# Block 1's second product ahead of block 0's feed-forward, and block 0's tokens turned by VectorE and DMAs

## The chip, the cores and the metric

The kernel runs on one core of a Trainium2 chip. Its time is the device time of that core in microseconds (us), and the time given is a median of several runs. A profiled execution gives a span, which is the time between the first and the last event on the core, and a trace of each instruction.

The core's engines are named as in the profile. PE is TensorE, with PEld for its weight loads. DVE is VectorE. ACT is ScalarE. POOL is GpSimd. SP is SyncE, and it only issues DMAs. ACT issues some DMAs too. A name with q (SPq, ACTq) is the queue of DMA issues of that engine. [...]

## The reference, cut to what matters

```
emb = silu(t) @ ada_w + ada_b
shift_msa, scale_msa, gate_msa, shift_mlp, scale_mlp, gate_mlp = split(emb, 6)
norm  = ln(x) * (1 + scale_msa) + shift_msa
x     = x + gate_msa * (gelu(norm @ ssm_w1 + ssm_b1) @ ssm_w2 + ssm_b2)
norm2 = ln(x) * (1 + scale_mlp) + shift_mlp
x     = x + gate_mlp * (gelu_tanh(norm2 @ ff_w1 + ff_b1) @ ff_w2 + ff_b2)
```

x is 2 x 2048 tokens of 512 features, in float32. ssm_w1 and ssm_w2 are 512 x 512, ff_w1 is 512 x 1024 and ff_w2 is 1024 x 512. ada_w is 512 x 3072. t has one row per batch, so the shifts, scales and gates are one vector per batch.

## The kernel before

**Blocks and stages.** The 4096 tokens are cut into eight blocks of 512. A block i passes four products on PE. hA_i is norm @ ssm_w1 with its GELU (`First`). oA_i is the product with ssm_w2 and the addition to x (`residual`). hC_i is norm2 @ ff_w1 with its GELU (`Second`). oC_i is the product with ff_w2 and the second addition to x, again through `residual`.

**Seven products instead of eight.** Every one of these multiplications is done by a Strassen-Winograd scheme on quarters of the operands. The seven products are called P1 to P7, and the function `group` issues them in the order P1, P2, P6, P5, P7, P3, P4. For a few early stages the order is `FIRST`, that is P1, P2, P5, P6, P7, P3, P4. Several products accumulate into one PSUM bank: P1, P6, P7 and P4 share bank y, P5 and P3 share bank v, and P2 has bank x. VectorE has to read a bank between two of them, by the addition in `residual` or in `hidden`. So PE can't start P6 before VectorE has read P1, nor P7 before it has read P6, nor P4 before P7, nor P3 before P5.

**Sums.** The scheme needs sums of quarters. They are steps on operands in SBUF:

- the sums of normalized tokens, written to tiles nS (`Norm.summed`, lines 319 to 322)
- the sums of hidden values, hSA for hA and hSC for hC (lines 309 to 312)
- the sums of weights, w_s and fw_s, which are also lines 309 to 312 for first operands and 319 to 322 for second ones. The weights w2 and fw2 are first multiplied by the gate (line 353, "fold").

The blocks 1 to 7 do hC in another way, called `products`: 26 products in place of 28, from 28 operands made of ff_w1 (the list HK_A, 37 steps on VectorE) and 24 operands made of the tokens (the list HK_B, 20 steps on POOL, the tile forms). Both lists are worked out by line 635. The list HK_A is worked out once, after hC_0 has read the plain weights and they have been loaded again. I call its steps the fw sums, and the 20 others the forms.

**Tokens on their way to PE.** A product needs features on partitions, while x has tokens there. Statistics come from VectorE (lines 419 and 420), the scales from eight small POOL steps (lines 428 to 446), and the normalization from ACT (line 459). Then there are two ways to turn the tokens. In the first, PE transposes them into PSUM (line 488) and ACT or VectorE applies shift and scale (lines 502 and 504). In the second, VectorE transposes blocks of 32 x 32 (`turn`, line 470), sixteen DMAs move the blocks (`move`, line 479), and ACT applies shift and scale to what arrived. In the kernel before, block 0's tokens go the first way for hA_0 and hC_0, block 1's for hA_1. All others go the second way.

**Order.** The order on each engine is the order of the code. Side work is put into `hooks`: a dictionary that lists, for a product such as P5, the steps to emit after it. The order of the stages on PE is

```
hA_0, oA_0, hA_1, hC_0, oA_1, oC_0, hA_2, products(1), oA_2, oC_1, hA_3, products(2), ...
```

Biases (line 610) are additions of a bias row to x on POOL. `load_x`, `load_ada` and `load_w` put loads on SP's queue, but the second load of ff_w1 is on ACT's. Large tiles (x, nT, hA, hC and the ada weights) share eight buffers.

Of the kernel before, what the change touches and what calls it, by code (L numbers as in the profile page):

```python
# [140 lines left out]
def kernel(  # L141
# [111 lines left out]
    def modulation(g0, part):  # L253


        g = g0 + part
        pa = ps_g.tile([P, D], F32, tag="x", name=f"pada_{g}")
        w = ada[g].rearrange("p k (n m q) -> p k m n q", n=KD, q=G)
        for k in range(KD):
            for m in range(P // G):  # L260
                nc.tensor.matmul(
                    pa[m * G : (m + 1) * G, :P],
                    silu[:, k, :],
                    w[:, k, m],
                    start=(k == 0),
                    stop=(k == KD - 1),
                    tile_position=(0, m * G),
                    skip_group_check=True,
                )
        turned = work.tile([P, KD, G], F32, tag="turned", name=f"turned_{g}")  # L270
        nc.vector.transpose(turned.rearrange("p n q -> p (n q)"), pa[:, :P])
        m = const.tile([P, KD, B], F32, tag=f"mod_{g0}_{part}", name=f"mod_{g0}_{part}")
        bias = colsT[:, R_ADA + g * KD : R_ADA + (g + 1) * KD]
        nc.vector.tensor_tensor(m, turned[:, :, :B], bias.unsqueeze(2).to_broadcast([P, KD, B]), ALU.add)
        mods[g0, part] = m
# [130 lines left out]
    class Norm:  # L406
# [68 lines left out]
        def move(self, engs=(nc.sync,)):  # L475

            for a in range(C):
                for m in range(C):
                    engs[m % len(engs)].dma_start(
                        out=self.nT[m * Q : (m + 1) * Q, a, :],  # L480
                        in_=self.bl[a * Q : (a + 1) * Q, m].rearrange("p k c q -> p (k c q)"),
                    )
# [174 lines left out]
    class Second:  # L657
# [9 lines left out]
        def products(self, fa, fb, hooks):  # L667
# [13 lines left out]
            def dest(d):  # L681
                f, col = d // 2, d % 2
                h = (self.lo, self.hi)[f // 2]
                return h[:, 2 * (f % 2) : 2 * (f % 2) + 2, col * HT : (col + 1) * HT]
# [9 lines left out]
            for n, (b, fresh, ra, rb, reads) in enumerate(HK_P):  # L694
# [9 lines left out]
                for d, sign in reads:  # L704
                    if d not in fresh_dest:
                        op = ALU.add if sign > 0 else ALU.subtract
                        nc.vector.tensor_tensor(dest(d), dest(d), ps[b], op)  # L707
                for d, sign in reads:
                    if d in fresh_dest:
                        nc.scalar.activation(dest(d), ps[b], AF.Identity, scale=float(sign))  # L710
                        fresh_dest.discard(d)
# [119 lines left out]
    hook(hooks, ("P1",), st[2:] + [n1[1].scales] + fold2(7, 8))  # L831
    hook(hooks, ("P2",), hA_sums[2:] + [lambda c=c: n1[1].normal(c, on_pe=True) for c in range(C)])
# [4 lines left out]
    hook(hooks, ("P3",), st[:2])  # L837
    residual("oA_0", 0, hA[0], w2_ops, KD // 2, hooks, order=FIRST)
    fw1_ops, fw1_sums, fw1_s = weight_of_first("fw1", fw1_sb)
    run(fw1_sums)  # L840
    n1_sums = n1[1].summed(nc.vector)
    run(n1_sums[:3])

    hooks = {}
    hook(hooks, ("P1",), st[2:] + [n2[0].scales])
    hook(hooks, ("P2",), [lambda c=c: n2[0].normal(c, on_pe=True) for c in range(C)])
    hook(hooks, ("P2",), biases(1, gb[2]))
    hook(hooks, ("P5",), n1_sums[3:])
    hook(hooks, ("P6",), [lambda: rows_of_gates(5)])
    hook(hooks, ("P3", "P3", "P4", "P4"), n2[0].turned((1, 3)))  # L850
# [19 lines left out]
    first_hooks = {}  # L870
    hook(first_hooks, ("P1",), [ff_gate])
    hook(first_hooks, ("P1", "P2"), n2_sums[2:])
    hook(first_hooks, ("P6", "P5", "P7", "P3"), fold5(0, 4))
    fold = None


# [3 lines left out]
    fb, fa_sums = {}, []  # L880
# [6 lines left out]
    n1[2] = Norm(2, 1)  # L887
    for i in range(NBLK):
        nxt, nx2, last = i + 1 < NBLK, i + 2 < NBLK, i + 1 == NBLK
        hC = Second(i)  # L890
        if i == 0:
            hooks = first_hooks
            hook(hooks, ("P2",), hA[1].summed(nc.gpsimd))
            hook(hooks, ("P2", "P3", "P4"), n1[2].stats())
            hC.group(0, n2[0].ops, hooks)
            hooks = {}
            hook(hooks, EARLY, hC.summed(0, nc.gpsimd))
            hook(hooks, ("P1",), [n1[2].scales])
            hook(hooks, EARLY, [lambda c=c: n1[2].normal(c) for c in range(C)])
            hook(hooks, ("P7", "P3", "P3", "P4"), [lambda c=c: n1[2].turn(c) for c in range(C)])  # L900
            hook(hooks, ("P4",), [n1[2].move])
            hook(hooks, ("P1", "P2", "P6", "P5"), fold5(4, 8))
            hook(hooks, ("P7",), fold5(8, 12) + [gb5_0] + biases(0, gb[5]))
            hC.group(1, n2[0].ops, hooks)
            fw2_ops = found["fw2"][0]
        else:
            hooks = {}
            if i == 1:
                hook(hooks, range(0, 26), take(len(fa_sums)))
            if i == 1:  # L910
                hook(hooks, (0,), [n1[i + 2].scales])
            if nxt:
                hook(hooks, (1, 2, 3, 4), hA[i + 1].summed(nc.gpsimd))
            hook(hooks, (6, 7, 8, 9), biases(i, gb[5]))
            if nx2:
                hook(hooks, (12, 14, 16, 18), [lambda c=c: n1[i + 2].normal(c) for c in range(C)])
                hook(hooks, (14, 16, 18, 20), [lambda c=c: n1[i + 2].turn(c) for c in range(C)])
                hook(hooks, (20,), [n1[i + 2].move])
            if fold:
                hook(hooks, (2, 6, 23, 25), fold[:4])  # L920
            hook(hooks, (20,), hC.summed(0, nc.gpsimd))
            hC.products(fa, fb[i], hooks)
# [3 lines left out]
        if nxt:  # L926

            if i == 0:
                hook(hooks, ("P1",), [lambda: load_w("fw1", fw1, fw1_sb, nc.scalar)])
                fa_sums.extend(sums_of_registers(HK_A, fa, (nc.vector,)))  # L930
# [24 lines left out]
        if i == 0:  # L955
            hook(hooks, ("P1",) * 6 + ("P5",) * 7 + ("P7",) * 7 + ("P3",) * 2, take(22))
        elif i + 3 < NBLK:
            hook(hooks, ("P5", "P7", "P3", "P4"), n1[i + 3].stats())
            hook(hooks, ("P4",), [n1[i + 3].scales])
# [11 lines left out]
        if nxt:  # L971
            hook(hooks, ("P7",) if nx2 else ("P5",), n2[i + 1].moved((None,) if nx2 else (None, nc.vector)))
# [34 lines left out]
        if i == 0:  # L1007
            hook(hooks, ("P5", "P7", "P3", "P4"), n1[i + 3].stats())
            hook(hooks, ("P1", "P2", "P2", "P6", "P5", "P7", "P3"), take(7))
# [50 lines left out]
```

## Time and profile before

| | |
|---|---|
| median of 3 runs | 608.73 us |
| lowest and highest | 607.0 and 609.22 us |
| profiled execution, its own time | 607.58 us |
| its span | 605.8 us |
| granted TensorE clock | 1.0 over the whole span |
| PE busy | 593.8 us, 98% |
| VectorE busy | 370.9 us, 61% |
| POOL busy | 394.7 us, 65% |
| ACT busy | 214.8 us, 35% |

The profiled execution is 1.15 us shorter than the median, and its time is 1.8 us more than its span. In the profile a group of instructions is written as line, engine, operation, out<-in with the shape, a count, then the busy time, the mean of one in ns, and the idle time before it with what ended it. In a timeline a row starts with its start and its duration in us. A matmul of this kernel is counted twice in the profile, so a product of four matmuls shows as x8. The tile names leave numbers out: fw stands for ff_w1 and ff_w2, w for ssm_w1 and ssm_w2, forms for the tile of token sums.

### The profile page before, as it was taken

The page shows a single profiled execution, that of the slowest core. Times are in us where ns is not written, and L with a number is a line of the kernel's source. Part 1 is how long each engine was busy: PE and PEld are TensorE (multiplying, and loading weights), DVE is VectorE, ACT ScalarE, POOL GpSimd, SP SyncE. Part 2 cuts the span into 40 slices and gives each one's busy share as a digit, 9 for nine tenths or more (in the row PEclk, how much of TensorE's full clock was granted, in tenths as well). Part 3 has the DMA queues.
Part 4 walks back from the last instruction along what each step waited for, and adds up shares of the span by engine and source line. Part 5 has one row for each costly group of instructions (what it writes and reads, how often), then busy time and mean ns, then how long its engine had stood idle before and what let it go on. Part 6 is the DMA issues. An engine that isn't in the chain of part 4 may idle for free.

```text
span 605.8 us, 8128 instructions
## 1 busy us (share of the span) xinstructions
PE 593.8 (98%) x2843; PEld 511.2 (84%) x2843; DVE 370.9 (61%) x638; ACT 214.8 (35%) x355; POOL 394.7 (65%) x446
## 2 busy tenths in 40 slices
PE   7999999999999999999999999999999999999997
PEld 4777888887888888888888888888888888888886
DVE  5987786799754375555754458644565346457642
ACT  3233340424622354323631346113553234212420
POOL 2876489889635797539978398885984695540110
PEclk9999999999999999999999999999999999999999
DMA  8980006410133103440042511321020300012001
GB/s 324 413 341 1 1 19 206 124 69 1 45 96 87 54 2 79 148 136 4 1 138 64 185 50 28 112 70 70 1 61 10 104 36 0 1 46 94 1 0 70
DMA packets 22604, 49.85 MB, mean 82 GB/s; under 512 B 4084, under 2 KB 4640, under 8 KB 21668
## 3 DMA queue, kind: packets, MB, share of 16 engines
q1 hardware_dynamic: 19264, 43.53, 21.3%
q10 hardware_dynamic: 3300, 5.80, 3.5%
q8 instruction: 23, 0.38, 0.3%
q14 instruction: 17, 0.14, 0.1%
HBM read 27.29 MB, written 8.39 MB: 59 GB/s over the span
## 4 chain that ended last, share of the span: by engine, by line
PE 86%; DVE 8%; DMA 2%; issue 1%; ACTq 1%; ACT 1%; POOL 0%; SPq 0%; DVEq 0%
PE py_oC L385 15%; PE px_hC L696 9%; PE py_oA L385 9%; PE py_hA L385 8%; PE pv_hC L696 8%; PE pv_oC L385 7%; PE py_hC L696 7%; PE pv_oA L385 4%; PE pv_hA L385 4%; PE px_oC L385 4%; PE py_hC L385 2%; PE px_oA L385 2%; PE px_hA L385 2%; DMA ada<-in_L_cond_ada_w_dram 2%; PE pv_hC L385 1%
## 5 line engine op out<-in xcount | busy, mean ns | idle before, releaser
L610 POOL TENSOR_TENSOR x<-x,gb 128x512 f32<-128x512 f32 x64 | 80.1, 1285 | 5.9 <-issue 2.1
L502 ACT ACTIVATE nT<-nT,mod,mod 128x512 f32<-128x512 f32 x50 | 36.7, 802 | 123.1 <-DMA nT<-blocks 114.7
L428 POOL TENSOR_SCALAR ve<-mv 128x4 f32<-128x4 f32 x16 | 3.8, 236 | 86.5 <-DVE mv L420 80.4
L459 ACT ACTIVATE nT<-x,nmr,rstd 128x512 f32<-128x512 f32 x52 | 39.6, 803 | 54.7 <-POOL nmr L446 38.9
L385 PE MATMUL py_oC<-fw_s,hSC 128*128 128x256 f32 x256 | 57.9, 379 | 0.0
L385 PEld LDWEIGHTS py_oC<-fw_s,hSC 128*128 128x128 f32 x256 | 48.6, 190 | 6.6
L309 POOL TENSOR_TENSOR hSC<-hClo 128x512 f32<-128x512 f32 x15 | 19.1, 1277 | 48.7 <-ACT hClo L691 38.9
L419 DVE BATCH_NORM_STATS2 st<-x 128x6 f32<-128x512 f32 x64 | 43.4, 677 | 5.0 <-DMA x<-in_x_dram 4.7
L598 DVE TENSOR_TENSOR x<-py_oC,x 128x512 f32<-128x512 f32 (+1 forms) x36 | 22.6, 630 | 37.6 <-PE py_oC L385 37.2
L696 PE MATMUL py_hC<-forms,fw 128*128 128x256 f32 x168 | 41.1, 380 | 0.0
L707 DVE TENSOR_TENSOR hClo<-hClo,py_hC 128x512 f32<-128x512 f32 x42 | 28.6, 681 | 16.9 <-ACT hClo L710 9.1
L470 DVE STREAM_TRANSPOSE blocks<-nT 128x512 f32<-128x512 f32 x52 | 35.2, 694 | 5.2 <-ACT nT L459 4.8
L635 POOL TENSOR_TENSOR forms<-forms 128x256 f32<-128x256 f32 x48 | 35.8, 747 | 2.8
L696 PEld LDWEIGHTS py_hC<-forms,fw 128*128 128x128 f32 x168 | 31.8, 190 | 4.7 <-DVE hClo L707 0.4
L598 DVE TENSOR_TENSOR x<-py_oA,x 128x512 f32<-128x512 f32 x32 | 22.1, 690 | 21.2 <-PE py_oA L385 19.6
L707 DVE TENSOR_TENSOR hChi<-hChi,pv_hC 128x512 f32<-128x512 f32 x35 | 23.3, 683 | 16.9 <-PE pv_hC L696 16.9
L385 PE MATMUL py_oA<-w_s,hSA 128*128 128x256 f32 x128 | 30.4, 380 | 0.8 <-DVE hSA L311 0.8
L385 PE MATMUL py_hA<-nS,w_s 128*128 128x256 f32 x128 | 30.4, 380 | 0.6 <-DVE hA L559 0.6
L691 ACT ACTIVATE hClo<-hClo,colsT 128x256 f32<-128x256 f32 x56 | 25.3, 500 | 13.6 <-DVE hClo L707 13.5
L385 PE MATMUL py_oC<-fw_s,hChi 128*128 128x256 f32 x128 | 29.0, 380 | 0.6 <-DVE x L598 0.6
L385 PE MATMUL px_oC<-fw,hChi 128*128 128x256 f32 x128 | 28.9, 379 | 0.0
L385 PE MATMUL pv_oC<-fw,hSC 128*128 128x256 f32 x128 | 28.9, 379 | 0.0
(224 smaller groups left out, 1426.0 us busy)
## 6 DMA issues: line engine op xcount, KB each, us to landing
nT<-blocks SPq DMA_DIRECT2D x152, 64.0 KB, 2.0
out_dram<-x SPq DMA_DIRECT2D x15, 512.0 KB, 3.0
x<-in_x_dram SPq DMA_DIRECT2D x7, 1024.0 KB, 6.3
ada<-in_L_cond_ada_w_dram SPq DMA_DIRECT2D x6, 1024.0 KB, 9.5
fw<-in_L_cond_ff_w_dram SPq DMA_DIRECT2D x3, 2048.0 KB, 9.3
nT<-blocks ACTq DMA_DIRECT2D x56, 64.0 KB, 2.2
w<-in_L_cond_ssm_w_dram SPq DMA_DIRECT2D x3, 1024.0 KB, 8.4
fw<-in_L_cond_ff_w_dram ACTq DMA_DIRECT2D x1, 2048.0 KB, 9.6
```

Of the source, the lines that this page charges most:

```text
L309: lambda: eng.tensor_tensor(s[1], q["11"], q["21"], ALU.subtract),
L385: nc.tensor.matmul(ps[b][j * apart][:, j, :], lhs(p, j, k), rhs(p, j, k), start=(fresh and j * (not apart) == 0 and k == 0), stop=(p in (" ...
L419: nc.vector.bn_stats(st, xs[self.i][:, c, :])
L459: nc.scalar.activation(t, x_c, AF.Identity, bias=self.nmr[:, c : c + 1], scale=self.rstd[:, c : c + 1])
L470: nc.vector.transpose(self.bl[:, :, :, c, :].rearrange("p m k q -> p k m q"), self.nT[:, c, :].rearrange("p (k m q) -> p k m q", k=KD, m=C),)
L502: nc.scalar.activation(dst, src, AF.Identity, bias=shift, scale=scale)
L598: nc.vector.tensor_tensor(d, ps[BANK[p]][:, js], d, ALU.add)
L610: lambda c=c: nc.gpsimd.tensor_tensor(xs[i][:, c, :], xs[i][:, c, :], gb, ALU.add)
L635: eng.tensor_tensor(reg[d], reg[a], reg[b], ALU.add if f == "+" else ALU.subtract)
L691: nc.scalar.activation(h, h, AF.Gelu_apprx_tanh, bias=fb1T[:, m : m + 1])
L696: nc.tensor.matmul(ps[b][:, j, :], fa[ra][:, j * P : (j + 1) * P], fb[rb].rearrange("p a (c q) -> p c a q", q=Q), start=(fresh and j == 0) ...
L707: nc.vector.tensor_tensor(dest(d), dest(d), ps[b], op)
```

## The change

The order of the first stages on PE becomes

```
hA_0, oA_0, hA_1, oA_1, hC_0, hA_2, oC_0, products(1), oA_2, oC_1, hA_3, products(2), ...
```

so oA_1 precedes hC_0, and hA_2 precedes oC_0. Block 0's second tokens go the second way: VectorE turns them in hA_1, SP and ACT issue eight moves each, and ACT applies shift and scale in oA_1. Their sums nS go from VectorE to POOL. The side work of these stages is hooked anew: two of the four ff_w1 sums on POOL run in oA_0 and the other two behind block 1's biases in hA_1. The statistics of block 1 for its second normalization run in hC_0, the multiplication of ff_w2 by its gate runs in hC_0 too, and its sums on POOL in hA_2. The second load of ff_w1 is issued at the start of hA_2, and of the 37 fw sums 4 are in hA_2, 29 in oC_0 and the last 4 in products(1). Before, 22 were in oC_0, 7 in hA_2 and 8 in products(1).

There are three smaller edits. `modulation` lets VectorE write the turned rows into PSUM instead of SBUF. `products` has a parameter `last`: in the last block ACT takes its fresh reads of a bank before VectorE's. And in the last block the shift and scale of the four token parts is hooked behind P5 and P7 in turn, where all four were behind P5.

```diff
-        turned = work.tile([P, KD, G], F32, tag="turned", name=f"turned_{g}")
-        nc.vector.transpose(turned.rearrange("p n q -> p (n q)"), pa[:, :P])
+        turned = pa[:, P : 2 * P]
+        nc.vector.transpose(turned, pa[:, :P])
+        turned = turned.rearrange("p (n q) -> p n q", n=KD)
...
-        def move(self, engs=(nc.sync,)):
+        def move(self, engs=(nc.sync,), part=range(C)):
...
-                for m in range(C):
+                for m in part:
...
+                fresh_reads = [r for r in reads if r[0] in fresh_dest]
+                other_reads = [r for r in reads if r not in fresh_reads]
+                fresh_dest -= {d for d, _ in fresh_reads}
+                for turn in (fresh_reads, other_reads)[:: 1 if last else -1]:
...
-    hook(hooks, ("P1",), st[2:] + [n1[1].scales] + fold2(7, 8))
-    hook(hooks, ("P2",), hA_sums[2:] + [lambda c=c: n1[1].normal(c, on_pe=True) for c in range(C)])
+    hook(hooks, ("P1",), hA_sums[2:3] + st[2:] + [n1[1].scales] + fold2(7, 8))
+    hook(hooks, ("P2",), hA_sums[3:] + [lambda c=c: n1[1].normal(c, on_pe=True) for c in range(C)])
...
+    fw1_ops, fw1_sums, fw1_s = weight_of_first("fw1", fw1_sb)
+    hook(hooks, ("P2",), fw1_sums[:1])
+    hook(hooks, ("P5",), fw1_sums[1:2])
     residual("oA_0", 0, hA[0], w2_ops, KD // 2, hooks, order=FIRST)
-    fw1_ops, fw1_sums, fw1_s = weight_of_first("fw1", fw1_sb)
-    run(fw1_sums)
     n1_sums = n1[1].summed(nc.vector)
-    run(n1_sums[:3])
+    run(st[2:3] + n1_sums[:2] + st[3:])
     hooks = {}
-    hook(hooks, ("P1",), st[2:] + [n2[0].scales])
-    hook(hooks, ("P2",), [lambda c=c: n2[0].normal(c, on_pe=True) for c in range(C)])
-    hook(hooks, ("P2",), biases(1, gb[2]))
-    hook(hooks, ("P5",), n1_sums[3:])
+    hook(hooks, ("P1",), n1_sums[2:3] + [n2[0].scales])
+    hook(hooks, ("P2",), n1_sums[3:] + [lambda c=c: n2[0].normal(c) for c in range(C)])
+    hook(hooks, ("P2",), biases(1, gb[2]) + fw1_sums[2:])
     hook(hooks, ("P6",), [lambda: rows_of_gates(5)])
-    hook(hooks, ("P3", "P3", "P4", "P4"), n2[0].turned((1, 3)))
+    hook(hooks, ("P6", "P6", "P7", "P7"), [lambda c=c: n2[0].turn(c) for c in range(C)])
+    hook(hooks, ("P7",), [lambda: n2[0].move((nc.sync,), (0, 1))])
...
+    n2[0].move((nc.scalar,), (2, 3))
+    hA_sums = hA[1].summed(nc.vector)
+    run(hA_sums[:2])
+    n1[2] = Norm(2, 1)
+    st = n1[2].stats()
+    hooks = {}
+    hook(hooks, ("P1",), hA_sums[2:3])
+    hook(hooks, ("P2",), hA_sums[3:])
+    hook(hooks, ("P2", "P6", "P6", "P5"), st)
+    hook(hooks, ("P5",), [n1[2].scales])
+    hook(hooks, ("P6",), n2[0].moved())
+    hook(hooks, ("P5",), [ff_gate])
+    hook(hooks, ("P7",), n2[0].summed(nc.gpsimd) + [lambda c=c: n1[2].normal(c) for c in range(C)])
+    turns = [lambda c=c: n1[2].turn(c) for c in range(C)]
+    residual("oA_1", 1, hA[1], w2_ops, KD // 2, hooks)
+    hC = Second(0)
...
+    hook(hooks, ("P1",), [gb5_0] + biases(0, gb[5]))
+    hook(hooks, ("P1", "P1", "P2"), turns)
+    hook(hooks, ("P2",), [n1[2].move])
+    hook(hooks, ("P3", "P4"), fold5(0, 2))
+    hC.group(0, n2[0].ops, hooks)
+    hooks = {}
+    hook(hooks, ("P1", "P1", "P2", "P6"), hC.summed(0, nc.gpsimd))
+    hook(hooks, ("P2",), n1[2].moved())
+    hook(hooks, ("P6",), n1[2].summed(nc.gpsimd))
+    hook(hooks, ("P1", "P2", "P6", "P5"), n2[1].stats())
+    hook(hooks, ("P5",), [n2[1].scales])
+    hook(hooks, ("P1", "P2", "P6", "P5", "P7", "P3"), fold5(2, 8))
+    hC.group(1, n2[0].ops, hooks)
...
+    hook(hooks, ("P1",), [lambda: load_w("fw1", fw1, fw1_sb, nc.scalar)])
+    hook(hooks, ("P1",), fold5(8, 12) + hC.summed(1, nc.gpsimd))
+    hook(hooks, ("P2", "P6", "P6", "P5"), [lambda c=c: n2[1].normal(c) for c in range(C)])
+    hook(hooks, ("P5", "P7", "P3", "P4"), [lambda c=c: n2[1].turn(c) for c in range(C)])
+    hook(hooks, ("P4",), [lambda: n2[1].move((nc.sync, nc.scalar))])
+    hook(hooks, ("P3", "P3", "P4", "P4"), take(4))
+    hA[2] = First(2, n1[2].ops, hooks)
...
+    hook(hooks, ("P1",), [lambda: load_x(3)] + take(5))
+    hook(hooks, ("P1",), n2[1].moved() + biases(2, gb[2]))
+    fb[1] = n2[1].registers()
+    hook(hooks, ("P2", "P6"), sums_of_registers(HK_B, fb[1], (nc.gpsimd,)))
+    hook(hooks, ("P2",) * 6 + ("P6",) * 5 + ("P5",) * 6 + ("P7",) * 4 + ("P3",) * 3, take(24))
+    hook(hooks, ("P5", "P7", "P3", "P4"), n1[3].stats())
+    residual("oC_0", 0, hC, fw2_ops, KH // 2, hooks)
...
-            hook(hooks, ("P7",) if nx2 else ("P5",), n2[i + 1].moved((None,) if nx2 else (None, nc.vector)))
+            moved = n2[i + 1].moved((None,) if nx2 else (None, nc.vector))
+            hook(hooks, ("P7",) if nx2 else ("P5", "P7", "P5", "P7"), moved)
```

## The prediction

> **What bounds the kernel now.** I read the page's busy shares and its chain first, then who made TensorE (PE) wait, then the engines' timelines over the first 175 us, which is where the change lies.
>
> ```profile
> PE 593.8 (98%) x2843; PEld 511.2 (84%) x2843; DVE 370.9 (61%) x638; ACT 214.8 (35%) x355; POOL 394.7 (65%) x446
> PE 86%; DVE 8%; DMA 2%; issue 1%; ACTq 1%; ACT 1%; POOL 0%; SPq 0%; DVEq 0%
> ```
>
> PE is the bound; only its own work and its waits count. The waits (line, waited-for, us in total, times, longest):
>
> ```profile
> PE py_oA L385 <- DVE hSA L311: 0.8, 1, 0.8
> PE px_hC L696 <- DVE hChi L707: 0.7, 2, 0.5
> PE px_hC L696 <- ACT hClo L710: 0.7, 1, 0.7
> PE pv_hA L385 <- DVE nT L320: 0.6, 1, 0.6
> PE py_oC L385 <- DVE x L598: 0.6, 1, 0.6
> PE py_hA L385 <- DVE hA L559: 0.6, 1, 0.6
> ```
>
> All but the ACT one and one of px_hC (the last block, 560 us) fall before 150 us. So little can be won: these waits and the PE transposes. PE's timeline (start, us):
>
> ```profile
> 59.55 1.07 PE L488 MATMUL pt<-ident,blocks 128*128 128x128 f32 x8
> 60.46 1.89 PE L385 MATMUL py_hA<-nS,w 128*128 128x256 f32 x8
> 62.19 1.04 PE L488 MATMUL pt<-ident,blocks 128*128 128x128 f32 x8
> 63.06 1.89 PE L385 MATMUL py_hC<-nT,fw 128*128 128x256 f32 x8
> ```
>
> Start to start, a product of hA, oA or hC takes 1.73 us (oC 3.45), and block 0's second transposes 0.91 + 0.87 = 1.78 us. What can be lost is seen where VectorE (DVE) and GpSimd (POOL) both read two operands from SBUF:
>
> ```profile
> 46.99 2.36 POOL L312 TENSOR_TENSOR fw_s<-fw,fw_s 128x1024 f32<-128x1024 f32 x1
> ```
>
> ```profile
> 47.66 2.24 DVE L319 TENSOR_TENSOR nS<-nT 128x512 f32<-128x512 f32 x1 [1.08 <-ACT nT L502]
> ```
>
> ```profile
> 113.98 5.49 POOL L610 TENSOR_TENSOR x<-x,gb 128x512 f32<-128x512 f32 x4
> ```
>
> ```profile
> 114.27 0.69 DVE L598 TENSOR_TENSOR x<-pv_oC,x 128x512 f32<-128x512 f32 x1 [1.62 <-PE pv_oC L385]
> 114.87 2.07 DVE L635 TENSOR_TENSOR fw_s<-fw_s,fw 128x256 f32<-128x256 f32 x2
> 116.97 1.37 DVE L635 TENSOR_TENSOR fw_s<-fw,fw_s 128x256 f32<-128x256 f32 x1
> 118.38 1.37 DVE L635 TENSOR_TENSOR fw<-fw,fw_s 128x256 f32<-128x256 f32 x1
> 119.79 0.42 DVE L635 TENSOR_TENSOR fw<-fw 128x256 f32<-128x256 f32 x1
> ```
>
> The DVE step on nS (0.69 alone) ended when POOL's did. Of the fw sums DVE got one done per POOL instruction, and 0.42 us once POOL was idle; a read from PSUM (L598, 0.69) was not held.
>
> **Early part.** The instruction order of both kernels gives DVE's sequence; I move the starts of the trace by it. In oA_0 the third DVE sum of hA (L311) goes ahead of two statistics: the 0.94 us gap before P6 goes, but block 1's scales, and with them its four normalizations on ACT (38.50 to 41.43), come 0.6 later, so PE waits at the first transpose instead and is 0.5 late there. POOL no longer runs the fw1 sums at 47 us, so nS is free by 49.5: the 0.80 gap before pv_hA goes (net -0.3), and DVE has read P6's bank by 54.7, when PE is still at the gate's rows (53.9 to 54.8): the 0.84 gap before P7 goes (net -1.1). Without the transposes hA_1 ends at 60.0 instead of 63.06: **-3.0**. The turn of the four ada modulations in PSUM costs PE nothing (their L274 takes 0.17 us alone, 1.15 and 2.37 beside POOL; what waits next there is ACT or the lock anyway).
>
> **The new tokens' path.** Statistics end at 50.4, POOL's scales take 3.2, ACT normalizes 53.6 to 56.5, DVE turns (0.65 each) until 58.8. Then 16 moves, half on SP, half on ACT. The issue rows:
>
> ```profile
> 89.19 14.27 SPq L479 DMA_DIRECT2D nT<-blocks  x16
> 112.67 5.23 SPq L479 DMA_DIRECT2D nT<-blocks  x8
> 159.04 10.44 SPq L479 DMA_DIRECT2D nT<-blocks  x16
> ```
>
> ACT's eight queue behind the last GELU of hA_1 (61.1); 5.4 of issue and 1.7 to land give 68.2, four modulations 71.2. hC_0 starts 13 us after 60.0 (oA_1's seven products and the gate's 0.86), so PE isn't held: no charge; late by over 4 us it would be one for one. The Trainium skill ("VectorE: DVE Perf Modes", Rules for kernel authors) says to transpose 128x128 on TensorE where PSUM will do. By it the change loses a 12 us path for 1.78 us of PE; by the rows that path is covered here, and the 1.78 is won. SP's x_2 load is now ahead of these moves, unblocked earlier, and free.
>
> **oA_1.** Its P6 needs two DVE sums of hA_1 after u2's GELU at 60.1. POOL, after biases (53.6 to 58.5), now runs the two late fw1 sums, 2.4 us each, until 63.3. One DVE step per POOL step: the first ends 61.5, the second 64.5, then an addition and the third sum, 65.8, against 63.5 wanted: **+2.3** (0 without the lock). hC_0: POOL's sums of nT reach s0 at 78.85, PE 78.8, and DVE has 2.0 us of work per 1.73 us product in group 1: +0.3.
>
> **hA_2 and oC_0, the main term.** Block 2's 16 moves leave on SP at 81.7, 11.8 us to modulation (as at 159: 171.1), 93.5 to 96.5. In order, POOL then has: sums of nT (to 101.9), scales of block 1 (105.1), the fw2 sums, 4 x 2.4 (114.9), four hSC sums (120.8), four biases (126.5), 20 forms at 0.86 (143.8; before 16.57 us in all). PE runs hA_2 from 99.8 to 111.9 and would end oC_0 at 136. So POOL is never idle in it, and DVE now has 33 fw sums there (4 in hA_2, 5 behind oC_0's P1, then 6, 5, 6, 4, 3), 22 before. These are ahead of the additions (L598) which read PSUM before PE may accumulate into the bank again. Rows of these sums:
>
> ```profile
> L635 DVE TENSOR_TENSOR fw<-fw 128x256 f32<-128x256 f32 x11 | 7.7, 696 | 0.0
> L635 DVE TENSOR_TENSOR forms<-forms 128x256 f32<-128x256 f32 x8 | 3.4, 421 | 0.2
> ```
>
> The third field is busy time in us and the mean in ns. Two totals can be made. By the mean row, 0.70 each, 15 sums from 111.4 and three other steps (1.9) put the addition of P6 at 123.8, before P7 wants the bank at 125.7; the next eleven, an addition and a statistic put that of P7 at 133.8, P4 wanting 132.6: **+1.2**. By the Trainium skill ("SBUF — State Buffer", Who interferes with whom): a DVE instruction with two SBUF inputs contends with a GpSimd one that reads SBUF, and the loser waits out the winner's whole instruction; so one sum per POOL step, 2.45, 1.37 or 0.86 us each. Laid side by side: two sums wait out fw2 steps (115.3), then a turn; two go with hSC steps 1 and 2, P1's addition ends at 119.0 (P6 wants the bank at 118.8, +0.3); five go with hSC 3, 4 and biases 1 to 3 (125.4), P2's addition, six with bias 4 and forms 1 to 5 (131.3), so P6's addition ends at 131.9 (P7 wants it at 126.0, **+6.0**); five with forms 6 to 10, P5's addition 136.2 (P3: +0.9); six with forms 11 to 16 (140.8), a statistic, P7's addition 142.2 (P4: 139.7, **+2.5**). Together +9.7. I take this: the mean row mixes free and held sums, and the timeline above has the strict form wherever POOL was busy. Both ends stay in the range. The fw1 load, now issued by ACT at 101, lands 9.6 later (its row's median), just before DVE's first fw sum at 111.4; what it is later, DVE is later.
>
> Gone in exchange is the 0.76 gap before the last oC_0 product and 0.2 of smaller ones: -1.0. products(1) then starts at 145.7 (137.41 before: -3.0 + 2.3 + 0.3 + 9.7 - 1.0 = +8.3). Its own stalls were 1.9; DVE is late into it: 2 to 3.5, +1.0.
>
> **The last block.** ACT reads a fresh bank before DVE: ACT no longer waits for hChi (its 0.60 at 560.04 starts near 557.5), and half the modulations move behind P7's addition, in DVE's idle time, so forms end 0.6 sooner. The gaps of 0.82 and 0.45 at 560 to 562 go: **-1.2**; at worst one stays.
>
> **Sum.** +8.3 + 1.0 - 1.2 = +8.1. The profiled execution took 607.58 (span 605.8), 1.15 under the median 608.73: 615.7 on the one, 616.8 on the other; I say **616**.
>
> **Rivals.** *(1) Strict lock*, above: 616, own range 612 to 620. *(2) The lock bites partly*: nT of block 1 comes later than 126, POOL idles before the forms and DVE clears its sums at 0.42: with oC_0 stalls of 4 to 5 the sum is +2.4 to +3.4, with the mean row's 1.2 it is -0.4: 606 to 612. *(3) DVE's backlog doesn't reach PE*: -3.0 + 2.3 + 0.3 - 1.0 - 0.5 (fewer stalls in products) - 1.2 = -3.1, and near -5.5 without oA_1's hold: 603 to 605.6. For it: the transposes are sure, and a sum takes 0.42 where POOL idles; against it: the four held rows at 114 us. It decides if P6's addition ends within 3.45 us of P6's end. *(4) The moves are late*: 14.3 for 16 on SP, as at 89 us beside the fw load: nT sums reach s0 1.6 us after hA_2's P6 wants it, and POOL's whole queue follows, about +10: 618 to 620; against it, the fw1 load is now behind these moves.
>
> **Chances.** 0.5% (3.0 us) is about what a measurement tells from no change. (1) 0.56 and (4) 0.08 make slower 0.64; (2) 0.18; (3) 0.18. The range 604 to 620 leaves out a little over half of (3) and the upper edge of (4); most of the chance lies in 612 to 620.
>
> **What would show it.** Right: PE waits of several us on py_oC before P7 and P4 of the first oC, released by DVE's L598 addition; DVE's fw sums there near 0.9 to 1.4 us; a 2 us wait of py_oA for hSA near 64 us; no px_hC wait in the last block. Wrong: fw sums near 0.42 in oC_0, or the first oC without gaps; then it is faster, and the POOL queue was free where I have it full.

## The result and the profile after

The changed kernel took 616.74 us (median; 614.97 to 617.31), the kernel before 607.90 beside it on the same chip. The ratio is 1.0139, 95% interval 1.0107 to 1.0170. The change costs 1.4%. The profiled execution of the changed kernel took 614.97 us with a span of 613.2, against 607.58 and 605.8 before. The three other runs, 616.3 to 617.31 us, had a mean granted clock of 0.992 and the profiled one 0.994, so what follows is read from a run that is 1.8 us under the median.

The page's busy shares, then its chain:

```profile
PE 594.4 (97%) x2827; PEld 510.8 (83%) x2827; DVE 379.0 (62%) x641; ACT 216.6 (35%) x357; POOL 394.6 (64%) x445
PE 84%; DVE 10%; issue 2%; DMA 2%; POOL 1%; ACT 1%; SPq 0%; POOLq 0%; DVEq 0%; ACTq 0%
```

PE issues 16 matmul rows fewer (the transposes) and is still the bound. But the span grew by 7.4 us while its busy time grew by 0.6, and VectorE's part of the chain went from 8% to 10%. So nearly all of the time went into waits. PE's waits, in the columns used for the kernel before:

```profile
PE py_oC L386 <- DVE x L599: 7.4, 3, 5.6
PE py_oA L386 <- DVE hSA L312: 2.0, 1, 2.0
PE px_hC L698 <- ACT hClo L712: 0.8, 1, 0.8
PE py_hC L386 <- POOL nS L322: 0.2, 1, 0.2
```

The first line is the addition of oC_0 (L599 now, L598 before). PE's timeline shows where the 7.4 us are. The rows are P6, P5, P7, P3 and P4 of oC_0:

```profile
119.58 3.69 PE L386 MATMUL py_oC<-fw_s,hSC 128*128 128x256 f32 x16 [0.21 <-DVE x L599]
123.11 3.62 PE L386 MATMUL pv_oC<-fw,hClo 128*128 128x256 f32 x16
132.28 5.33 PE L386 MATMUL py_oC<-fw_s,hSC 128*128 128x256 f32 x16 [5.55 <-DVE x L599]
137.44 3.62 PE L386 MATMUL pv_oC<-fw,hSC 128*128 128x256 f32 x16
142.74 3.72 PE L386 MATMUL py_oC<-fw_s,hChi 128*128 128x256 f32 x16 [1.68 <-DVE x L599]
```

P7 waits 5.55 us for P6's addition and P4 1.68 us for P7's. P7 itself also takes 5.16 us from its start to P3's, where the other products take 3.45 to 3.55. VectorE's rows ahead of P6's addition, which is the L599 at 131.54, and the two additions after it, P5's at 135.94 and P7's at 142.02:

```profile
121.69 2.79 DVE L636 TENSOR_TENSOR fw_s<-fw_s,fw 128x256 f32<-128x256 f32 x2
124.51 1.38 DVE L636 TENSOR_TENSOR fw_s<-fw,fw_s 128x256 f32<-128x256 f32 x1
125.81 0.68 DVE L599 TENSOR_TENSOR x<-px_oC,x 128x512 f32<-128x512 f32 x1
...
127.34 0.83 DVE L636 TENSOR_TENSOR fw<-fw 128x256 f32<-128x256 f32 x1
...
130.68 0.94 DVE L636 TENSOR_TENSOR fw<-fw 128x256 f32<-128x256 f32 x1
131.54 0.68 DVE L599 TENSOR_TENSOR x<-py_oC,x 128x512 f32<-128x512 f32 x1
...
135.94 0.68 DVE L599 TENSOR_TENSOR x<-pv_oC,x 128x512 f32<-128x512 f32 x1
...
142.02 0.66 DVE L599 TENSOR_TENSOR x<-py_oC,x 128x512 f32<-128x512 f32 x1
...
146.40 0.41 DVE L636 TENSOR_TENSOR fw<-fw_s,fw 128x256 f32<-128x256 f32 x1
```

POOL's rows of the same time:

```profile
121.33 5.69 POOL L611 TENSOR_TENSOR x<-x,gb 128x512 f32<-128x512 f32 x4
126.98 0.90 POOL L636 TENSOR_TENSOR forms<-nT 128x256 f32<-128x256 f32 x1
127.96 0.79 POOL L636 TENSOR_TENSOR forms<-nT,forms 128x256 f32<-128x256 f32 x1
```

Read the two side by side. Beside a bias of 1.4 us a sum of fw parts takes 1.4 us, beside a form of 0.8 to 0.9 it takes 0.83 to 0.94, and after POOL's last form (144.4) it takes 0.41. The additions, which read PSUM, keep their 0.68. They come late only because they stand behind the sums in VectorE's queue: P6 had ended by 123.3, and its addition started at 131.54, after the six sums that stand between P2's addition and it in the code.

The smaller wait, of P6 in oA_1 for the sum hSA, has the same form. VectorE's two sums ahead of it, which take 0.69 alone, and POOL's rows of that time:

```profile
59.85 1.70 DVE L310 TENSOR_TENSOR hSA<-hA 128x512 f32<-128x512 f32 x1 [0.70 <-ACT hA L568]
61.58 2.72 DVE L311 TENSOR_TENSOR hA<-hA 128x512 f32<-128x512 f32 x1
```

```profile
58.63 2.37 POOL L312 TENSOR_TENSOR fw_s<-fw 128x1024 f32<-128x1024 f32 x1
61.08 2.67 POOL L313 TENSOR_TENSOR fw_s<-fw,fw_s 128x1024 f32<-128x1024 f32 x1
```

Last, the stretches of the wait, of P7, and of what follows. The field after the engines' busy times is PE's granted clock:

```profile
126.60:132.30 5.70, 0.15 (x2) 0.02 (x1) 5.60 (x8) 0.05 (x1) 5.54 (x8) 0.69 0.00 0
132.30:137.50 5.20, 5.20 (x17) 4.32 (x18) 5.13 (x8) 0.00 (x0) 4.96 (x7) 0.69 0.00 0
137.50:142.70 5.20, 3.56 (x17) 2.79 (x15) 5.06 (x9) 0.00 (x0) 5.04 (x8) 1.00 0.00 0
```

P7 ran at a granted clock of 0.69, and 3.45 / 0.69 = 5.0 us is nearly all of its 5.16.

### The profile page after: what moved, and what is told of

It is laid out like the page before. It is cut to its first block, busy times and chain, and to the rows that moved or that the text cites. A ratio compares the mean times of both kernels' runs of the same rounds, so it can differ in the third digit from the quotient of the medians.

```text
span 613.2 us, 8130 instructions
## 1 busy us (share of the span) xinstructions
PE 594.4 (97%) x2827; PEld 510.8 (83%) x2827; DVE 379.0 (62%) x641; ACT 216.6 (35%) x357; POOL 394.6 (64%) x445
## 4 chain that ended last, share of the span: by engine, by line
PE 84%; DVE 10%; issue 2%; DMA 2%; POOL 1%; ACT 1%; SPq 0%; POOLq 0%; DVEq 0%; ACTq 0%
PE py_oC L386 16%; PE px_hC L698 9%; PE pv_oC L386 8%; PE pv_hC L698 8%; PE py_hA L386 8%; PE py_hC L698 7%; PE py_oA L386 7%; PE pv_hA L386 4%; PE px_oC L386 4%; PE pv_oA L386 4%; DVE fw_s L636 2%; PE px_hA L386 2%; PE py_hC L386 2%; DVE fw L636 2%; PE px_oA L386 2%
## 5 line engine op out<-in xcount | busy, mean ns | idle before, releaser
L503 ACT ACTIVATE nT<-nT,mod,mod 128x512 f32<-128x512 f32 x54 | 39.6, 803 | 115.4 <-DMA nT<-blocks 115.4
L386 PE MATMUL py_oC<-fw_s,hSC 128*128 128x256 f32 x256 | 59.6, 387 | 5.8 <-DVE x L599 5.8
L460 ACT ACTIVATE nT<-x,nmr,rstd 128x512 f32<-128x512 f32 x56 | 42.4, 803 | 55.7 <-POOL nmr L447 39.9
L599 DVE TENSOR_TENSOR x<-py_oC,x 128x512 f32<-128x512 f32 (+1 forms) x36 | 22.5, 628 | 39.9 <-PE py_oC L386 39.9
L471 DVE STREAM_TRANSPOSE blocks<-nT 128x512 f32<-128x512 f32 x56 | 37.9, 694 | 3.9 <-ACT nT L460 3.4
L715 DVE TENSOR_TENSOR hClo<-hClo,py_hC 128x512 f32<-128x512 f32 x42 | 28.5, 681 | 17.0 <-ACT hClo L712 9.4
L599 DVE TENSOR_TENSOR x<-py_oA,x 128x512 f32<-128x512 f32 x32 | 22.1, 690 | 20.5 <-PE py_oA L386 19.9
L715 DVE TENSOR_TENSOR hChi<-hChi,pv_hC 128x512 f32<-128x512 f32 x35 | 23.4, 684 | 17.1 <-PE pv_hC L698 17.1
L386 PEld LDWEIGHTS py_oA<-w_s,hSA 128*128 128x128 f32 x128 | 24.2, 190 | 6.2 <-DVE hSA L312 2.4
L386 PE MATMUL pv_oC<-fw,hClo 128*128 128x256 f32 x128 | 28.9, 379 | 0.0
```

Of the source, the lines that this page charges most:

```text
L386: nc.tensor.matmul(ps[b][j * apart][:, j, :], lhs(p, j, k), rhs(p, j, k), start=(fresh and j * (not apart) == 0 and k == 0), stop=(p in (" ...
L460: nc.scalar.activation(t, x_c, AF.Identity, bias=self.nmr[:, c : c + 1], scale=self.rstd[:, c : c + 1])
L471: nc.vector.transpose(self.bl[:, :, :, c, :].rearrange("p m k q -> p k m q"), self.nT[:, c, :].rearrange("p (k m q) -> p k m q", k=KD, m=C),)
L503: nc.scalar.activation(dst, src, AF.Identity, bias=shift, scale=scale)
L599: nc.vector.tensor_tensor(d, ps[BANK[p]][:, js], d, ALU.add)
```

## The experiments

My theory: the fw sums on VectorE are held by GpSimd's steps, one for one, and hold up oC_0's additions. Rivals: VectorE simply has too many steps in these stages; or something else of the new order (the moved tokens, the forms, the order of stages) is late. The ratios below are to runs of the kernel before on the same chip (medians of 607.06 to 607.90 us). Starts of the whole first part differ by up to 2 us between profiles, with the first loads, so stages are compared by their length.

| run | median us | ratio (95%) | oC_0 us | products(1) us | the 37 sums on VectorE, us |
|---|---|---|---|---|---|
| changed kernel | 616.74 | 1.0139 (1.0107 to 1.0170) | 33.99 | 24.05 | 32.5 |
| without the sums | 604.71 | 0.9953 (0.9936 to 0.9970) | 24.17 | 23.08 | (8 left) |
| without GpSimd's work beside them | 604.45 | 0.9943 (0.9922 to 0.9964) | 24.94 | 22.46 | 22.0 |
| the sums in other places (respread) | 613.76 | 1.0102 (1.0084 to 1.0120) | 25.30 | 32.01 | 33.2 |
| fw1's last two sums earlier | 613.83 | 1.0110 (1.0089 to 1.0131) | 33.79 | 24.03 | 32.3 |
| block 2's biases earlier | 613.34 | 1.0097 (1.0081 to 1.0113) | 29.79 | 23.98 | 28.3 |
| four moves at once | 611.85 | 1.0093 (1.0079 to 1.0106) | 25.19 | 30.37 | 27.7 |
| the small edits, old order | 606.30 | 0.9987 (0.9981 to 0.9994) | | | 24.9 |
| the kernel before, early part mended | 606.07 | 0.9991 (0.9979 to 1.0003) | | | 27.4 |
| the same, and four sums earlier | 604.69 | 0.9967 (0.9952 to 0.9983) | | | 26.5 |
| GpSimd's work moved away | 606.70 | 1.0002 (0.9993 to 1.0011) | 26.56 | 24.07 | 25.1 |

oC_0 is from its first matmul to the first of products(1), and products(1) to the first of oA_2. Without a wait they are 7 x 3.45 = 24.2 and 26 x 0.864 = 22.5 us. The last column adds up VectorE's fw rows from 98 to 165 us; the kernel before has 24.8 there, and 37 at 0.42 would be 15.5. The three runs without entries for the stages are made from the kernel before, whose stages stand in another order.

### Without the sums

```diff
-    hook(hooks, ("P1",), [lambda: load_x(3)] + take(5))
+    take(29)
+    hook(hooks, ("P1",), [lambda: load_x(3)])
...
-    hook(hooks, ("P2",) * 6 + ("P6",) * 5 + ("P5",) * 6 + ("P7",) * 4 + ("P3",) * 3, take(24))
```

> Leaves out 29 of the 33 sums of fw parts that VectorE makes in oC_0 (the 4 of hA_2 stay), so the products read unsummed parts. If these sums, slowed beside GpSimd, are what holds oC_0's additions, all four waits go with them: P6 0.38, P7 5.72, P4 1.85, and P7's own slow matmuls (5.16 us instead of 3.45) too if the low granted clock follows from the 5.7 us pause. products(1) starts at about 136.6 us in place of 146.3, and the time falls by 9.7 to about 607.0. If the clock was low for another reason, P7 still takes about 5.2 us and the time is about 608.7. If something else of the new order were late (block 1's moved tokens, the forms, hSC), a wait of several us would stay somewhere before products(1), and the time would stay above 611.

All the waits of oC_0 went, and P7 took 3.45 us: the stage is 24.17 us, 9.82 less. products(1) lost another 1.0. The median, 604.71, is 2.3 under what I had expected. So nothing else of the new order makes oC_0 wait: not the moved tokens, the forms or hSC. It does not tell whether the sums are too many or too slow.

### Without GpSimd's work beside them

```diff
+    hook(hooks, ("P2",), [lambda: nc.gpsimd.memset(forms[:, 8:], 0.0)])     # in hC_0
...
-    hook(hooks, ("P1",), n2[1].moved() + biases(2, gb[2]))
+    hook(hooks, ("P1",), n2[1].moved())
...
-    hook(hooks, ("P2", "P6"), sums_of_registers(HK_B, fb[1], (nc.gpsimd,)))
```

> Leaves out GpSimd's biases of block 2 and its 20 forms in oC_0 and clears the forms' tile earlier instead; all 33 fw sums stay on VectorE in their order. If the sums hold PE because GpSimd's steps hold them, each sum after 121.3 us (when the hSC sums end) takes 0.41 us instead of 0.83 to 1.49, P2's addition comes at about 123 instead of 125.8, P6's at about 126.3 instead of 131.5, P7's wait falls from 5.7 to about 0.3, P4's goes, the clock stays full: about 9 us less, about 607.7. If VectorE simply has too many steps in its queue, 29 sums and 7 additions whatever GpSimd does, P7's wait stays near 5 us and the time at 614 to 617.

VectorE does every sum here, and the time is that of the run without sums: 604.45 against 604.71. Two of VectorE's rows, from the stretch in which the changed kernel's took 0.83 to 1.4:

```profile
125.24 0.42 DVE L636 TENSOR_TENSOR fw<-fw 128x256 f32<-128x256 f32 x1
125.58 0.42 DVE L636 TENSOR_TENSOR fw_s<-fw,fw_s 128x256 f32<-128x256 f32 x1
```

And the only wait that is left in oC_0, beside that of oA_1:

```profile
PE py_oA L386 <- DVE hSA L312: 2.0, 1, 2.0
PE py_oC L386 <- DVE x L599: 0.4, 1, 0.4
```

This tells the two apart. It is not the number of VectorE's steps but their length beside GpSimd's. I had expected 607.7. By the profiles the gain is 9.9 us: 9.05 in oC_0, 1.59 in products(1), which ran its 22.46 us without a wait, and small pieces, less 1.67 of a low clock in oA_1. The medians differ by 12.3, and what makes up the difference isn't shown.

### The same sums in other places

```diff
-    hook(hooks, ("P1",), [lambda: load_x(3)] + take(5))
+    hook(hooks, ("P1",), [lambda: load_x(3)] + take(2))
...
-    hook(hooks, ("P2",) * 6 + ("P6",) * 5 + ("P5",) * 6 + ("P7",) * 4 + ("P3",) * 3, take(24))
+    hook(hooks, ("P2",) * 3 + ("P6",) * 3 + ("P5",) * 4 + ("P7",) * 5 + ("P3",) * 4 + ("P4",) * 4, take(23))
```

> The fw sums placed otherwise, none left out: after P1 2 (was 5), P2 3 (6), P6 3 (5), P5 4 (6), P7 5 (4), P3 4 (3), P4 4 (0), 8 in products(1) (was 4). At the rates of the changed kernel (1.4 us a sum until 127, 0.9 after) P2's addition comes at about 121.5 and P6's at about 126.3, so P7 waits 0 to 0.5 us; P4 0 to 1; the clock stays full. products(1) starts at about 137.5 to 138.3 and the time is about 608.5 (607.5 to 610). If the number of sums and not their place is the cause, the waits come back at P4 and in the products, and the time is 612 or more.

oC_0 behaved as I had worked out, 25.30 us, and the time hardly fell. products(1) grew by 8 us, almost what oC_0 had lost. Its large wait:

```profile
PE px_hC L698 <- ACT hClo L712: 4.6, 1, 4.6
```

Why was ScalarE late? Its row, and VectorE's row just before it:

```profile
149.03 0.60 ACT L712 ACTIVATE hClo<-px_hC 128x512 f32<-128x512 f32 x1 [8.18 <-POOL rstd L445]
```

```profile
148.25 0.68 DVE L715 TENSOR_TENSOR hChi<-hChi,px_hC 128x512 f32<-128x512 f32 x1
```

The profile names POOL's rstd as the releaser. I take it to be VectorE's L715. The code has it read this bank ahead of ScalarE's L712, and for the same copy in the kernel before the profile itself names that step (L707 there):

```profile
L710 ACT ACTIVATE hClo<-px_hC 128x512 f32<-128x512 f32 x21 | 12.5, 597 | 32.4 <-PE px_hC L696 23.1 <-DVE hChi L707 9.3
```

ScalarE started 0.1 us after L715's end here (148.93), in the changed kernel (152.59 and 152.68) and in the run with four moves below (147.06 and 147.15). In that run rstd had been done at 146.51, and the profile names another small POOL step, nmr, that ended at 147.11. So the ends alone don't decide it; by the code the cause is again VectorE, whose backlog now stood in front of products(1). In the products after the wait PE's clock was low, and they took about 3.3 us longer (see the last section); this is part of the 8 us. With the sums as slow as before (33.2 us for all 37), putting them elsewhere moved the wait. My expectation failed because I looked at the additions alone. A time over 612 was to speak for the number of the sums; the runs with GpSimd's work left out and moved away show that it is their length.

### fw1's last two sums earlier

```diff
-    hook(hooks, ("P5",), fw1_sums[1:2])
+    hook(hooks, ("P5",), fw1_sums[1:])
...
-    hook(hooks, ("P2",), biases(1, gb[2]) + fw1_sums[2:])
+    hook(hooks, ("P2",), biases(1, gb[2]))
```

> The last two fw1 sums are put on GpSimd right behind the second (44.7 us, where it was idle until 50.2) instead of behind the biases of block 1 (58.6 us). If their 2.4 and 2.7 us on GpSimd are what stretches the two hSA sums from 0.69 to 1.70 and 2.72 us and so P6 of oA_1, its 2.0 us wait goes, less up to 0.3 where the nS sums of block 1 now meet them: about 614.6. If P6 waits for P1's addition because the biases of block 1 or ScalarE's hA are late, the wait stays and the time is the same as the changed kernel's, 616.7.

The two sums of hA that took 1.70 and 2.72 us in the changed kernel, here:

```profile
60.95 0.69 DVE L310 TENSOR_TENSOR hSA<-hA 128x512 f32<-128x512 f32 x1 [0.70 <-ACT hA L568]
61.68 0.69 DVE L311 TENSOR_TENSOR hA<-hA 128x512 f32<-128x512 f32 x1
```

The 2.0 us wait is gone. The fw1 sums now met the first nS sum of block 1 instead (2.23 us, 0.69 in the changed kernel), and PE waited there:

```profile
PE pv_hA L386 <- DVE nT L321: 0.6, 1, 0.6
```

hA_1 is 1.18 us longer (14.46 against 13.28), oA_1 2.28 shorter (12.95 against 15.23). By the profiles products(1) starts 1.1 earlier; the ratio fell by 0.3 points.

### Block 2's biases earlier

```diff
-    hook(hooks, ("P6",), n1[2].summed(nc.gpsimd))
+    hook(hooks, ("P6",), biases(2, gb[2]) + n1[2].summed(nc.gpsimd))
...
-    hook(hooks, ("P1",), n2[1].moved() + biases(2, gb[2]))
+    hook(hooks, ("P1",), n2[1].moved())
```

> One move: GpSimd's four biases of block 2 go from oC_0 (121.3 to 127.0 us) to the second group of hC_0, where GpSimd was idle from 93.0 to 97.4. Nothing is left out, and VectorE's queue is as in the changed kernel. If GpSimd's steps hold the sums, those between 121.6 and 127 take 0.42 instead of 1.4 us, P6's addition comes at about 126.7 and P7 waits about 0.2 instead of 5.7 (and runs at the full clock). The sums beside the forms stay at 0.85, so P3 and P4 wait 1 to 2 and 2 to 3 us, and products(1) starts at about 141.5 instead of 146.3: about 612. If the number of VectorE's steps is the cause, nothing moves: 616.7.

Only GpSimd's queue changed. Its four biases ran at 92.9 us, and between 122 and 127 the sums took 0.42. P7 didn't wait. P4 did, and then ran slowly:

```profile
136.81 5.38 PE L386 MATMUL py_oC<-fw_s,hChi 128*128 128x256 f32 x16 [2.33 <-DVE x L599]
```

products(1) started at 142.02, 141.5 expected. The profiled execution took 610.63 us; the median, 613.34, is 1.3 over what I expected, and what made the difference isn't shown.

### Four moves at once

```diff
-    hook(hooks, ("P2",), biases(1, gb[2]) + fw1_sums[2:])
+    hook(hooks, ("P2",), fw1_sums[2:] + biases(1, gb[2]))
...
+    hook(hooks, ("P6",), biases(2, gb[2]) + n1[2].summed(nc.gpsimd))
...
-    hook(hooks, ("P2",) * 6 + ("P6",) * 5 + ("P5",) * 6 + ("P7",) * 4 + ("P3",) * 3, take(24))
-    hook(hooks, ("P5", "P7", "P3", "P4"), n1[3].stats())
+    hook(hooks, ("P5", "P7", "P3", "P3"), n1[3].stats())
+    hook(hooks, ("P2",) * 6 + ("P6",) * 3 + ("P5",) * 4 + ("P7",) * 4 + ("P3",) * 4 + ("P4",) * 3, take(24))
```

> The changed order with four moves and nothing left out: the biases of block 2 as in the run with the biases early; fw1's last two sums ahead of the biases of block 1 on GpSimd; the statistics of block 3 ahead of the fw sums of their stage; of the sums 3 (was 5) behind P6, 4 (6) behind P5, 4 behind P7, 4 (3) behind P3, 3 (0) behind P4. If the sums beside GpSimd are the whole cost of the new order, P6 of oA_1 waits 0 to 0.3 instead of 2.0, oC_0 1.5 instead of 9.7, products(1) as before about 1.5: about 606 (604.5 to 608), level with the kernel before or just under. If the delay only moves on (as it did when the sums were respread: there the products waited 8 us), the time stays above 610.

A miss. oC_0 took 25.19 us, but the rest of the backlog again reached products(1):

```profile
PE px_hC L698 <- ACT hClo L712: 4.0, 1, 4.0
```

In oA_1 the hSA sums met the biases in place of the fw1 sums, and P6 still waited 1.4. After the 4.0 us wait PE's clock was low, and the next products took 2.9 us longer (see the last section). Of the four moves, the earlier biases are the only one that took GpSimd's steps away from VectorE's in oC_0, and that wasn't enough.

### The small edits without the new order

In the kernel before, with the statement order of the rest untouched: the change's new `modulation` and `products` as they are in the changed kernel, and these two calls:

```diff
-            hC.products(fa, fb[i], hooks)
+            hC.products(fa, fb[i], hooks, last)
...
-            hook(hooks, ("P7",) if nx2 else ("P5",), n2[i + 1].moved((None,) if nx2 else (None, nc.vector)))
+            moved = n2[i + 1].moved((None,) if nx2 else (None, nc.vector))
+            hook(hooks, ("P7",) if nx2 else ("P5", "P7", "P5", "P7"), moved)
```

> The kernel before with the change's three small edits and without its new order: the modulation turned inside PSUM, ScalarE's copies ahead of VectorE's additions in the last block's products, the last block's modulation spread over P5 and P7. If the tail's gain is theirs, products(7) lose their waits and the time falls by 1.2 to about 606.2. If the tail got shorter only because the new order reaches it later or otherwise, it stays at 607.4.

The last block, from the start of products(7) to that of oC_7, takes 22.62 us in place of 23.82, with no wait. The gain of 1.2 in the last block belongs to these edits and not to the order; the medians show 0.8 (0.4 to 1.2). Which of the three edits makes it was not tried.

### The kernel before, with its early part mended

```diff
-    run(fw1_sums)
+    run(fw1_sums[:2])
...
-    hook(hooks, ("P2",), biases(1, gb[2]))
+    hook(hooks, ("P2",), fw1_sums[2:])
...
-            hook(hooks, ("P2",), hA[1].summed(nc.gpsimd))
+            hook(hooks, ("P2",), hA[1].summed(nc.gpsimd) + biases(1, gb[2]))
```

> As the kernel before with the three small edits, and besides: fw1's last two sums on GpSimd behind the scales in hA_1 (about 57 to 62 us) in place of block 1's biases, these in hC_0 behind the hA_1 sums. If GpSimd's fw1 sum at 47.0 us is what stretched the first nS sum to 2.24 us, hA_1's two waits (0.64 and 0.59) go and hC_0 starts at about 61.8 instead of 63.1; with the tail's 1.2 the time is about 605.0. If those sums then meet the nS sums of block 0, P6 of hC_0 waits up to 1 us and it stays at 606.

hC_0 started at 61.48 in place of 63.06, so the mechanism held. oC_0 gave it back: P4 waited 1.83 us for P7's addition, 0.6 in the kernel before, and the 37 sums took 27.4 us instead of 24.8. The time is 606.07 where I had expected 605.0, and no gain over the kernel before that is clear of the noise.

### The new order with GpSimd's work moved away from the sums

```diff
+    hook(hooks, ("P2",), fw1_sums[2:3] + biases(1, gb[2]))     # hA_1; fw1_sums[3:] behind nS in hC_0
+    hook(hooks, ("P4",), [ff_gate])                            # hA_1, was oA_1
...
+    hook(hooks, ("P2",), hA_sums[3:] + [gb5_0] + biases(0, gb[5]))                  # oA_1, was hC_0
+    hook(hooks, ("P5", "P7", "P7", "P3", "P3", "P4"), fold5(0, 8))                  # oA_1, was hC_0
...
+    hook(hooks, ("P3",), fold5(8, 12))                         # hC_0 group 0, was hA_2
...
+    hook(hooks, ("P1",), hC.summed(1, nc.gpsimd) + biases(2, gb[2]))                # hA_2
...
+    hook(hooks, ("P5", "P7", "P3", "P3"), n1[3].stats())
+    hook(hooks, ("P2",) * 9 + ("P6",) * 7 + ("P5",) * 4 + ("P7",) * 4, take(24))
```

> The changed order, nothing left out, with GpSimd's work moved to where VectorE has no step with two SBUF inputs: gate of fw2 made at the end of hA_1 and its eight folds on VectorE in oA_1, fw2's four sums on GpSimd in hC_0 (were at 105.8 to 115.7 us), block 0's ff biases in oA_1, block 2's biases behind hSC (about 111 to 116), one fw1 sum (needed last) behind the nS sums of block 0, block 3's statistics ahead of the fw sums, 24 sums in oC_0 as 9, 7, 4, 4 behind P2, P6, P5, P7. If GpSimd's steps beside the sums are the whole cost of the new order, the sums from 116 to 126 us take 0.42, VectorE is done with them by about 131, oC_0 waits 0 to 0.7 and products(1) 0 to 1.5, oA_1's P6 at most 0.5: about 604.5 to 606. If the number of VectorE's steps in the two stages still binds, a wait of 3 us or more is left in oC_0 or in the products: 609 or more.

606.70, level with the kernel before and 0.7 over the range that I had expected, but 1.4 points under the changed kernel, with the same steps on every engine. GpSimd had nothing to do from 118.7 to 126.9, and VectorE did 16 of the sums there at 0.42, where the changed kernel's took 0.83 to 1.4. Two POOL rows and one of the sums between them:

```profile
113.22 5.50 POOL L611 TENSOR_TENSOR x<-x,gb 128x512 f32<-128x512 f32 x4
126.86 0.72 POOL L636 TENSOR_TENSOR forms<-nT 128x256 f32<-128x256 f32 x1 [8.14 <-DMA x<-in_x_dram]
```

```profile
124.42 0.42 DVE L636 TENSOR_TENSOR fw_s<-fw,fw_s 128x256 f32<-128x256 f32 x1
```

The sums of oC_0, 29 as before, were also placed anew behind its products. Placing alone had not helped in the respread run, but how much it adds here was not tried. Its profiled execution took 608.74 us, with a low clock during the first loads (see the last section). The waits that are left:

```profile
PE py_hC L386 <- POOL nS L322: 1.4, 1, 1.4
...
PE py_oC L386 <- DVE x L599: 1.1, 1, 1.1
PE px_hC L698 <- ACT hClo L712: 0.9, 1, 0.9
...
PE pv_oC L386 <- DVE x L599: 0.7, 1, 0.7
```

### A version that beats both

The kernel before with its early part mended, and with four sums put into a stretch where VectorE stood idle beside GpSimd's steps of a few elements:

```diff
-            hook(hooks, ("P1",) * 6 + ("P5",) * 7 + ("P7",) * 7 + ("P3",) * 2, take(22))
+            hook(hooks, ("P1",) * 10 + ("P5",) * 4 + ("P7",) * 6 + ("P3",) * 2, take(22))
```

> The kernel before with the three small edits and the moved fw1 sums and biases of the earlier run, and 4 of oC_0's fw sums put behind P1 instead of P5 (10, 4, 6, 2 in place of 6, 7, 7, 2), where VectorE had nothing to do from 107.5 to 109.3 us and GpSimd had only steps of a few elements. P7's addition then comes at about 119.4 instead of 120.6, so that P4's 1.8 us wait goes: about 604.3. If VectorE is late there for another reason, 606 as before.

604.69 us, 0.33% under the kernel before (interval 0.17% to 0.48%). P4's wait fell to this:

```profile
PE py_oC L386 <- DVE x L599: 0.2, 1, 0.2
```

## Why the prediction was right, point by point

The forecast was 616.0 and slower; the median is 616.74, and by its own sum on the profiled execution 615.7 against 614.97. The change is +7.4 us by the profiles and +8.8 by the medians, with +8.1 foreseen; that 616 is so near the median is in part luck. Rival (1), the strict lock, is what happened. The steps:

| step | predicted | measured |
|---|---|---|
| end of hA_1 | -3.0 | -3.14 (59.92) |
| oA_1, P6 held | +2.3 | +2.18 |
| hC_0 and hA_2 | +0.3 | +0.66 |
| oC_0, P6 | +0.3 | +0.38 |
| oC_0, P7 | +6.0 | +5.72 |
| oC_0, P3 | +0.9 | 0 |
| oC_0, P4 | +2.5 | +1.85 |
| oC_0, slow clock in P7 | not foreseen | +1.71 |
| gaps of the kernel before gone (its oC_0 and hA_2: 37.23 us, 36.26 without a wait) | -1.0 | -0.97 |
| the remainder | | +0.49 |
| start of products(1) in all | +8.3 | +8.88 |
| products(1)'s own stalls | +1.0 | -0.28 |
| last block | -1.2 | -1.19 |

**Right, and shown by runs.** The main term: the strict form of the lock gave +9.7, the mean row +1.2; measured are 9.66. Taking GpSimd's steps away, with VectorE's kept, removed it, and so did moving them away. The signs that I had named are in the trace: the waits of P7 and P4 for L599, sums of 0.8 to 1.4 us there, the 2.0 us wait for hSA near 64 us, and no wait in the last block. The Trainium skill ("SBUF — State Buffer", Who interferes with whom) was the right one of the two totals to follow. oA_1's term is shown by the run with fw1's sums earlier, and the last block's by the small edits in the kernel before. The new tokens' path was covered, as charged: no wait of hC_0 for a modulation is in the trace, whose four end at 69.9, 5.2 us ahead of hC_0. So following the rule to transpose on TensorE took 1.78 us of PE there that the path gave back, by the rows; no run changed this alone.

**Right in sum, not in its parts on PE.** P3 waited for nothing, P4's wait was smaller, and P7's low clock, which I had left out, took 1.71 instead. That the sum still fits is not luck. VectorE sets it: its rows leave no idle time from 119.4 to 142.7, and the additions of P6, P5 and P7 ended at 132.22, 136.62 and 142.68, where I had 131.9, 136.2 and 142.2. P4 can't start before the last of them. At the full clock P7 would have ended at 135.7, and P3 would have waited 0.9 for P5's addition, as foreseen. So by these rows the low clock only filled time in which PE would have waited, and cost nothing here.

**The mis-sized term.** products(1) was to lose 1.0 more and lost 0.28 less. VectorE was late into it, as I said, but P4's wait had, as I read it, already let it catch up. The respread run shows what the term is when oC_0 doesn't wait: 8 us, a low clock included. The backlog was paid where PE first met it, and my sum charged part of it twice.

**Rivals.** (2) and (3) needed GpSimd idle beside the sums. GpSimd was not, in the changed kernel; in the run with its work moved it was, and the time came to 606.7, inside rival (2)'s range. (4), late moves, didn't happen: block 2's modulation was done at 97.3 us, ahead of hA_2 at 100.2.

**Left open.** The runs show that a sum and a GpSimd step end one for one when both read SBUF. They don't show the port itself. No run took the low clock away by itself. Two waits of 0.40 and 0.26 us make up the term of hC_0 and hA_2 (+0.66 for +0.3); what doubled it was not tried.

## What to carry to other kernels

When a stage order changes, lay the queues of VectorE and GpSimd side by side over the new stages and count one VectorE step with two SBUF operands per GpSimd step, not VectorE's busy share. If PE waits at one place because another queue is behind, moving steps along that queue moves the wait: make them shorter, here by giving GpSimd its work at a time when VectorE reads PSUM. A wait of a few us can also leave a low clock behind it, here up to 3.3 us more. And put a small edit into the kernel before by itself, since a gain of 1.2 us is easily lost in a loss of 9.

## What the runs showed of the hardware that I had not expected

**The clock after a wait.** PE's granted clock fell in or after waits of a few us. In the run with the sums respread the wait was 4.6 us; the two stretches after it:

```profile
149.70:153.10 3.40, 3.34 (x7) 2.26 (x8) 3.40 (x6) 1.29 (x2) 3.24 (x3) 0.50 0.00 0
153.10:156.50 3.40, 3.40 (x11) 2.67 (x11) 3.40 (x5) 1.07 (x3) 3.32 (x4) 0.60 0.00 0
```

Of the run with four moves, after a wait of 4.0:

```profile
147.80:151.20 3.40, 3.40 (x8) 2.75 (x9) 1.86 (x3) 1.27 (x2) 3.24 (x3) 0.50 0.00 0
151.20:154.60 3.40, 3.40 (x12) 2.71 (x12) 1.55 (x3) 1.52 (x3) 3.32 (x4) 0.66 0.00 0
```

Read in slices of 0.2 us, the clock is at half in one piece: for 6.8 us in these two runs, in the changed kernel (from 128.8, still in P7's wait, to 135.6) and in the run with fw1's sums earlier, and for 3.4 us in the run with the biases earlier. A product of 3.45 us took 5.16 after 5.55 us of waiting, 5.19 after 5.54 (fw1's sums earlier) and 5.21 after 2.33 (biases earlier). These fit half the clock for 3.4 us of the product: 3.4 + (3.45 - 1.7) = 5.15, an estimate from the rows. In the two runs above most of the 6.8 us fell after the wait: four products of 0.864 us took 6.80 and 6.36 us, 3.3 and 2.9 more.

The Trainium skill ("TensorE: Matmul & The Clock Gate", What's actually happening) says that the clock is halved after an idle window of about 3.4 us. The half agrees, but the waits can be shorter: 2.33 us, and 2.0 us in oA_1 in one profile (without GpSimd's work: P6 took 2.38 instead of 1.83 and P5 2.87 instead of 1.73), though not in the changed kernel's. In two profiles (without the sums; GpSimd's work moved away) it was at half for 3.4 us from about 11.5, around waits of 1.45 and 1.59 us for the first loads; the kernel before waited 1.44 there and kept 1.0. So the length of one wait alone doesn't decide it. Where it fell, PE lost up to 3.3 us beyond the wait, unless it would have waited anyway. In the pages of these profiles the clock's row is below 9 tenths only in the slices of such waits and of the first loads. No run changed the clock alone, so that the wait is its cause is argued, not shown.

**A releaser can be a neighbour.** The profile named GpSimd's rstd as what released ScalarE in two profiles and its nmr in a third. These ends fit within 0.1 us, and so do those of VectorE's L715, which reads the same PSUM bank, in all three. The name alone doesn't settle it: hold it against the code, and against what the profile names for the same step elsewhere, here VectorE in the kernel before.
